# Another order of the same instructions: a product with a relu and a residual on one core

## The chip, the cores and the metric

The kernel runs on one core of one Trainium2 chip. The metric is the device time of one execution in microseconds; a kernel's time is the median of its runs. A core has five engines with queues of their own: TensorE (PE; PEld are its weight loads), VectorE (DVE), ScalarE (ACT), GpSimd (POOL), and SyncE (SP), which here only issues transfers. Each engine works through its queue in the order in which the program was written; between engines, semaphores hold an instruction until what it needs is there.

## What is computed

x has the shape (4, 1024, 512), W is (1536, 512), all in 32-bit floats. Cut to what matters:

```python
hidden = concatenate([cond, cond], axis=-1)          # (4, 512)
x_mean = mean(x, axis=1, keepdims=True)              # over 1024 rows
fused = concatenate([x, x_mean * ones_L, hidden[:, None, :] * ones_L], axis=-1)
out = x + relu(einsum('bld,do->blo', fused, W) + b)
```

So each of the four batch rows needs a product of its 1024 x 512 values with the first third of W, plus one bias vector per batch row: its mean times the second third of W, its condition times the last third, and b.

## The kernel before

**Tiles.** x is 32 tiles of 128 rows, eight per batch row. A tile needs 12 products: four slices of the inner dimension (j = 0 to 3), each with three products, because the 32-bit product is made of rounded parts: hi of x times hi of W, lo of x times hi of W, hi of x times lo of W (hi is the value cast to a rounded type, lo the difference that the cast left). Tiles are prepared in ten units: units 0 and 1 are one tile each, unit 2 has two tiles, all others four. Unit 4 holds tiles 8 to 11, unit 9 tiles 28 to 31.

**The order.** The program is a list of some 700 names, `ORDER` (lines 22 to 49), and each name is a task of one or a few instructions; line 437 goes through the list and issues them. Since each engine takes its instructions in that order, the list sets every queue. A letter behind @ picks the engine: d VectorE, a ScalarE, p GpSimd. The list was made by a search over orders with a plan of the times (a planner outside the kernel). The names:

- `X0.0`, `W0`, `C`, `B`, `M`, `V`, `Z4.0`: transfers into the chip, issued by SyncE one by one (line 145). X are tiles of x by rows, W0 and W1 the two halves of the first third of W, M and V the other thirds, C the condition, Z a unit of x laid out for VectorE's transposes.
- `T0.1`: a transpose, unit 0, slice 1. Units 0 to 3 are transposed by TensorE (line 244), the others by VectorE from Z (line 246).
- `h0.1`, `l0.1`: hi (line 252, ScalarE) and lo (line 258) of x. `wh1r`, `wl1r`: hi (lines 215 and 217) and lo (line 221) of W, slice 1, right half; without l or r, both halves.
- `p0.1.2`: tile 0, slice 1, product 2 of the three (line 348); `p9.2` stands for all three; `p31.1l` for the left half of tile 31.
- `K`, `b`, `r`, `F`: for tiles 0 to 17 the result is evicted from its bank of PSUM (K, ScalarE at line 415, VectorE at 423), the bias added (b, GpSimd), relu taken (r, ScalarE) and x added (F, GpSimd at line 431). For tiles 18 to 31 the bias is written into the bank first (P, ScalarE at lines 402 and 382) and F takes relu and adds x in one VectorE operation (lines 406 and 386). `S` stores a tile.
- `to`, `m`, `f`, `fa`, `vh`, `vl`, `pb`, `bc`, `g`, `d`, `as`: the bias of a batch row. `to` sums on GpSimd, `m` are four VectorE products with M, `f` ScalarE's copy after them, `pb` a product that sums over partitions, `bc` its copy.
- `fill`: products on zeros that keep TensorE busy before the first data.

**What holds what.** There are five banks for results: tile t uses bank t mod 5 (po_136 to po_140 in the lists below), so tile t + 5 can start only after the eviction of tile t. x's slots, lo buffers and parked results are reused in the same way. TensorE reads hi and lo of W from `w_hi` and `w_lo`, which are made at the start, from W0 (slices 0 and 1) and W1 (slices 2 and 3).

The loop that issues the tasks, and a cast and a difference of W:

```python
        @task(f"wh{j}{h}")
        def _(e, j=j, d=d):
            src, dst = xs[W_SLOT][:, j, d], w_hi[:, j, d]
            if e == "a":
                nc.scalar.activation(dst, src, AF.Copy)
            else:
                nc_of[e].tensor_copy(dst, src)
...
    for name in ORDER:
        if name == "fill":
            fill()
            continue
        name, _, engine = name.partition("@")
        tasks.pop(name)(engine)
```

Of the kernel before, what the change touches and what calls it, by code (L numbers as in the profile page):

```python
# [19 lines left out]


ORDER = """
relu X0.0 W0 X0.1 X0.2 W1 C B fill fill fill fill fill fill T0.0 T0.3 X1.0 T0.1 T0.2 X1.1 h0.0 V h0.1 l0.0@d
wh1r@d wh1l@a l0.1@d wh0l@a wl1r@p Z4.0 Z4.1 fill fill fill p0.1.0 wh0r@d h0.2 wl1l@d p0.1.1 h0.3 wl0l@p
wl0r@d p0.0.0 T1.0 l0.3@d T1.1 T1.3 T1.2 p0.0.1 p0.1.2 h1.0 T2.2 Z4.2 Z4.3 h1.2 T2.3 l1.0@d T2.0 h1.1 l1.2@d
p0.0.2 h2.3 p1.0.1 wh3@d p1.1.0 h1.3 T2.1 wh2@d h2.2 p1.1.2 wl3@p p1.0.2 wl2@d h2.0 Mb p1.0.0 p0.3.0 h2.1 Ma
p0.2.0 l0.2@d p1.2.0 l2.3@d p0.3.1 Z5.2 Z5.3 t3 p1.3.0 l1.1@d p1.2.2 l2.0@d p0.2.2 t2 p0.2.1 l2.1@d p1.3.2
l2.2@d p1.1.1 p0.3.2 t1 l1.3@d p1.2.1 t0 p2.3 T3.1 T3.0 h3.1 T3.3 ac0@p T3.2 h3.0 l3.1@d Z5.0 Z5.1 p2.1 K0@a
ac1@p h3.3 p3.0 g0.0 l3.3@d p1.3.1 p3.3 K1@a l3.0@d d0.0 Z6.2 Z6.3 p2.2 h3.2 p5.0 g0.1 l3.2@d g1.0 p3.1 d0.1
p6.1 T4.0 Z6.0 Z6.1 p6.3 d1.0 as0 T4.3 h4.0 p4.1 to0 T4.1 p3.2 g2.0 p2.0 K3@a m0.0 p5.2 h4.3 m0.1 p4.3 g1.1  # L30
T4.2 h4.1 p5.1 d1.1 K2@a p5.3 m0.2 Z7.0 Z7.1 h4.2 p6.0 l4.3@p m0.3 Z7.2 Z7.3 p7.3 l4.0@d f0 l4.1@p l4.2@d p6.2
g2.1 fa0 p4.2 d2.0 T5.1 vh0 p4.0 K5@a p8.2 vl0 h5.1 p7.1 T5.3 K6@a l5.1@p p8.1 T5.0 h5.3 p8.0 d2.1 K4@a pb0
T5.2 p10.0 h5.0 l5.3@p bc0@a p7.2 l5.0@d Z8.2 Z8.3 h5.2 p9.2 T6.1 as1 to1 X3.0 p11.1 b0@p Z8.0 Z8.1 m1.0 p8.3
T6.0 X5.1 b1@p p10.2 X2.1 K8@a m1.1 p9.3 h6.1 b3@p l5.2@d p11.2 r1 m1.2 p7.0 l6.1@p T6.2 p10.3 K7@a p13.2 h6.0
m1.3 b2@p p9.1 h6.2 T6.3 f1 p10.1 b5@p fa1 Z9.0 Z9.1 h6.3 p11.0 T7.1 vh1 p9.0 l6.3@p r5 p11.3 vl1 h7.1 p12.0
l6.0@d K9@a l7.1@p l6.2@d p12.2 K10@a r2 T7.3 p12.3 r0 pb1 T7.2 K11@a p13.0 F0 h7.3 p12.1 T7.0 bc1@a b4@p
p15.2 h7.2 K12@d p14.3 h7.0 T8.1 as2 p14.1 to2 F2 r3 p15.0 m2.0 r4 p16.3 m2.1 r12 b7@p S2 p13.3 X3.1 m2.2 S0
p17.1 l7.3@p m2.3 Z9.2 Z9.3 p14.2 l7.0@d f2 X5.0 p17.0 F4 l7.2@d g3.0 X2.0 p13.1 fa2 F1 p17.3 T8.0 vh2 p14.0
h8.1 vl2 F5 h8.0 p15.3 K13@d r7 p16.0 T8.3 l8.1@p S5 p16.1 X4.1 K14@d pb2 S1 d3.0 p16.2 T8.2 bc2@a p15.1 P18
l8.0@d F3 p17.2 g3.1 P19 p18.2 K17@d h8.3 d3.1 S3 p18.0 T9.1 X4.0 P22 p19.2 h8.2 l8.3@p T9.0 p19.0 r17 h9.1  # L40
p22.2 l8.2@d b10@p as3 p19.1 K15@d X6.1 T9.2 p22.0 P20 b6@p h9.0 p18.1 T9.3 h9.2 p18.3 K16@d p22.3 h9.3 F18
p19.3 P21 to3 b8@p m3.0 r10 S18 p22.1 P23 X6.0 m3.1 p20.2 r6 b11@p m3.2 p20.1 r15 r14 p23.3 m3.3 F6 p20.0 F22
f3 p21.3 l9.1@p fa3 p21.1 F19 vh3 F17 p23.1 vl3 p20.3 F7 p23.0 F20 pb3 p21.0 l9.3@p S7 bc3@a S19 p21.2 P27 S17
p23.2 F15 P25 S4 F21 r16 p27.2 F23 S21 P24 p27.1 S6 r13 l9.2@d p27.0 r8 l9.0@d P28 p27.3 F8 p25.0 F27 F16
p28.0 S8 P31r S15 P26 p25.2 X7.1 F10 p31.1r S22 p31.3r X7.0 p24.0 F12 p24.3 p25.3 b9@p S12 p31.0r p31.2r p24.2
F14 r9 p25.1 p24.1 F13 S14 p26.2 S10 F24 p26.3 F9 F25 P29 p26.0 F31r S25 P30 p29.2 S9 S31r p26.1 S27 p28.2 S20
F26 S23 p28.3 S26 P31l r11 p28.1 S24 F11 p29.1 F28 p29.3 S11 p30.0 S13 p30.3 S16 S28 p30.1 p30.2 p29.0 F30
p31.0l F29 p31.1l S30 p31.3l p31.2l S29 F31l S31l
""".split()


# [418 lines left out]
```

## Time and profile before

| | us |
|---|---|
| median of three runs | 104.49 |
| lowest and highest of them | 104.44, 106.45 |
| the profiled execution, its own time | 105.26 |
| its span, from the first to the last instruction | 103.5 |

The profile is of one execution, and its span leaves out what lies around the program. The granted clock of TensorE was 1.000 as a mean over the span. A group's row of the page names the line, the engine, the operation and what it writes and reads, then its count, busy time, mean length in ns, and the idle time ahead of it with what ended that. Busy shares are means over the whole span, and the start, the long middle and the end have different limits, so the windows and the timeline are needed too.

### The profile page before, as it was taken

Reading aid. Unit: us, or ns where it says so; the run is one execution under the profiler, and the core shown is the slowest. Engines: PE = TensorE matmul, PEld = TensorE weight load, DVE = VectorE, ACT = ScalarE, POOL = GpSimd, SP = SyncE. Lnnn points to the kernel's source line nnn. Section 1 sums busy time; section 2 is a strip of 40 time slices with the busy share of each in tenths; the row PEclk is TensorE's granted clock in tenths of the full one; section 3 lists DMA queues with packets and bytes.
Section 4 is the critical chain, followed back from the end, with each engine's and each line's share of the span. In section 5 each row is a group of like instructions: output and inputs, shape, how many; then the busy total and the mean of one; then the engine's idle time right before and its main releaser. Section 6 shows DMA issues by size and latency. Waiting matters only on the chain.

```text
span 103.5 us, 1434 instructions
## 1 busy us (share of the span) xinstructions
PE 97.6 (94%) x441; PEld 78.5 (76%) x441; DVE 73.1 (71%) x112; ACT 61.5 (59%) x153; POOL 71.6 (69%) x72
## 2 busy tenths in 40 slices
PE   6969989999999999999999999999999999999950
PEld 2538659888888888888888888888888888888850
DVE  1086992679999999999999999989948200622240
ACT  5156407969867956899937799887469302430000
POOL 4050507783797999997899999959997999705000
PEclk9999999999999999999999999999999999999999
DMA  1999999999999999999996999969209839999982
GB/s 51 285 332 407 411 234 209 215 326 201 210 216 209 203 208 199 197 155 244 244 180 146 344 234 393 402 219 344 101 17 371 328 108 278 331 403 405 401 331 77
DMA packets 22657, 26.31 MB, mean 254 GB/s; under 512 B 1269, under 2 KB 13817, under 8 KB 22650
## 3 DMA queue, kind: packets, MB, share of 16 engines
q1 hardware_dynamic: 22650, 26.23, 95.1%
q8 instruction: 3, 0.05, 0.2%
q14 instruction: 4, 0.03, 0.1%
HBM read 17.83 MB, written 8.39 MB: 253 GB/s over the span
## 4 chain that ended last, share of the span: by engine, by line
PE 83%; DVE 6%; DMA 5%; issue 2%; ACT 1%; SPq 0%; DVEq 0%
PE po L348 79%; DMA x<-in_L_cond_W_dram 5%; DVE lo L258 3%; DVE w_hi L217 2%; PE px L244 2%; ACT hi L252 1%; PE acc L326 1%; DVE cT L266 1%; PE po L244 0%; PE acc L244 0%; DVE x L386 0%; SPq L145 0%; DVE w_lo L221 0%; DVEq L258 0%
## 5 line engine op out<-in xcount | busy, mean ns | idle before, releaser
L348 PE MATMUL po<-w_hi,hi 128*128 128x512 f32 (+1 forms) x132 | 50.4, 385 | 0.9 <-ACT w_hi L215 0.7
L348 PE MATMUL po<-w_hi,lo 128*128 128x512 f32 (+1 forms) x132 | 50.8, 385 | 0.0
L348 PE MATMUL po<-w_lo,hi 128*128 128x512 f32 (+1 forms) x132 | 50.5, 385 | 0.1
L348 PEld LDWEIGHTS po<-w_hi,hi 128*128 128x128 f32 x132 | 24.8, 188 | 6.8 <-ACT w_hi L215 1.2
L348 PEld LDWEIGHTS po<-w_hi,lo 128*128 128x128 f32 x132 | 24.8, 188 | 5.0 <-DVE lo L258 0.3
L348 PEld LDWEIGHTS po<-w_lo,hi 128*128 128x128 f32 x132 | 24.7, 188 | 5.1 <-DVE w_lo L221 0.5
L431 POOL TENSOR_TENSOR x<-o,x 128x512 f32<-128x512 f32 x18 | 23.0, 1293 | 4.9 <-ACT o L427 4.9
L406 DVE SCALAR_TENSOR_TENSOR x<-po,x 128x512 f32<-128x512 f32 x13 | 8.8, 688 | 15.8 <-PE po L348 15.8
L258 POOL TENSOR_TENSOR lo<-xT,hi 128x512 fp32r<-128x512 f32 x12 | 15.5, 1298 | 0.9 <-ACT hi L252 0.9
L258 DVE TENSOR_TENSOR lo<-px,hi 128x512 fp32r<-128x512 f32 (+1 forms) x22 | 11.5, 537 | 6.5 <-ACT hi L252 6.5
L252 ACT ACTIVATE hi<-px 128x512 fp32r<-128x512 f32 (+1 forms) x22 | 10.4, 474 | 8.9 <-PE px L244 8.5
L419 POOL TENSOR_TENSOR o<-o,bias 128x512 f32<-128x512 f32 x12 | 15.3, 1295 | 0.0
L246 DVE STREAM_TRANSPOSE px<-z 128x512 f32<-128x512 f32 x12 | 13.0, 1098 | 0.7 <-DMA z<-in_x_dram 0.7
L427 ACT ACTIVATE o<-o 128x512 f32<-128x512 f32 x18 | 10.6, 620 | 4.3 <-POOL o L419 4.3
L246 DVE STREAM_TRANSPOSE xT<-z 128x512 f32<-128x512 f32 x12 | 12.9, 1086 | 0.1
L302 DVE SCALAR_TENSOR_TENSOR acc<-w_mean,tot,acc 128x512 f32<-128x512 f32 x16 | 11.8, 740 | 0.6 <-POOL tot L293 0.3
L402 ACT ACTIVATE po<-bias 128x512 f32<-128x512 f32 x13 | 7.6, 592 | 2.8 <-DVE x L406 2.2
L252 ACT ACTIVATE hi<-xT 128x512 fp32r<-128x512 f32 x12 | 7.5, 625 | 1.2 <-DVE xT L246 1.2
L415 ACT ACTIVATE o<-po 128x512 f32<-128x512 f32 x12 | 7.0, 589 | 1.9 <-PE po L348 1.8
L221 POOL TENSOR_TENSOR w_lo<-x,w_hi 128x256 fp32r<-128x256 f32 (+1 forms) x3 | 2.9, 968 | 7.0 <-DVE w_hi L217 7.0
L284 POOL TENSOR_TENSOR cond<-cond,term 128x512 f32<-128x512 f32 x4 | 5.2, 1297 | 2.8 <-ACT term L280 2.8
L280 ACT ACTIVATE term<-wc,cT 128x512 f32<-128x512 f32 x8 | 5.6, 719 | 0.1
(51 smaller groups left out, 71.9 us busy)
## 6 DMA issues: line engine op xcount, KB each, us to landing
out_dram<-x SPq DMA_DIRECT2D x31, 256.0 KB, 4.7
x<-in_x_dram SPq DMA_DIRECT2D x15, 512.0 KB, 6.9
z<-in_x_dram SPq DMA_DIRECT2D x24, 256.0 KB, 10.2
x<-in_L_cond_W_dram SPq DMA_DIRECT2D x2, 512.0 KB, 5.9
x<-in_L_cond_W_dram SPq DMA_DIRECT2D x1, 1024.0 KB, 10.3
w_mean<-in_L_cond_W_dram SPq DMA_DIRECT2D x2, 512.0 KB, 8.9
x<-in_x_dram SPq DMA_DIRECT2D x2, 256.0 KB, 4.1
out_dram<-x SPq DMA_DIRECT2D x2, 128.0 KB, 3.4
```

Source lines behind the costliest of these rows:

```text
L246: nc.vector.transpose(xT.rearrange("p (n t) -> p n t", t=Q), zs[z_of(u)][:, : n * NQ].rearrange("p n (a j) -> p n j a", j=J)[:, :, j])
L252: nc.scalar.activation(his[buf][:, col : col + m], xT, AF.Copy, accum_out=sums[:, r, j, s : s + 1])
L258: nc_of[e].tensor_tensor(los[buf][:, col : col + m], xT, his[buf][:, col : col + m].bitcast(F32), ALU.subtract)
L280: nc.scalar.activation(terms[k], wc[:, k], AF.Copy, scale=cT[:, k, r : r + 1])
L302: nc.vector.scalar_tensor_tensor(acc, w_mean[:, j, :], tot[:, r, j : j + 1], acc, ALU.mult, ALU.add)
L348: nc.tensor.matmul(v, lhsT=a[:, col : col + P], rhs=m, start=WAYS[t] != "I" and key not in done, stop=done.count(key) == 3 * J - 1, skip_g ...
L402: nc.scalar.activation(bank(t), biases[r], AF.Copy)
L406: nc.vector.scalar_tensor_tensor(x_tile(t), bank(t), 0.0, x_tile(t), ALU.max, ALU.add)
L415: nc.scalar.activation(o, bank(t), AF.Copy)
L419: nc_of[e].tensor_tensor(o, o, biases[r], ALU.add)
L427: nc.scalar.activation(o, o, AF.Relu)
L431: nc.gpsimd.tensor_tensor(x_tile(t), o, x_tile(t), ALU.add)
```

## The change

No task is added, taken away or altered. The list is another one: a new search was run whose plan keeps VectorE's casts and lo of W apart from GpSimd's operations, lets W land later, and keeps TensorE cold for longer. The first two rows of the list:

```diff
 ORDER = """
-relu X0.0 W0 X0.1 X0.2 W1 C B fill fill fill fill fill fill T0.0 T0.3 X1.0 T0.1 T0.2 X1.1 h0.0 V h0.1 l0.0@d
-wh1r@d wh1l@a l0.1@d wh0l@a wl1r@p Z4.0 Z4.1 fill fill fill p0.1.0 wh0r@d h0.2 wl1l@d p0.1.1 h0.3 wl0l@p
+relu X0.0 W0 X0.1 X0.2 C W1 X1.1 fill fill fill fill fill fill T0.2 T0.0 B T0.3 T0.1 X1.0 h0.0 V h0.1 l0.0@d
+wh1r@d wh1l@a l0.1@d h0.2 Z4.2 Z4.3 fill fill fill p0.1.0 wl1l@d h0.3 wh0r@d p0.1.1 wh0l@a T1.0 wl0l@d T1.1
...
 """.split()
```

Of engines, these tasks change: `wl1r`, `wl0l` and `wl3` go from GpSimd to VectorE, and `wh3` from VectorE to ScalarE. All else that changes is place in a queue.

**VectorE, the start.** x_63 is where W0 and W1 land; lo_89 and lo_90 are those of units 0 and 1, px_141 and px_142 their transposes. Before:

```order
L258 TENSOR_TENSOR lo_89<-px_141,hi_75 128x128
L217 CAST w_hi<-x_63 128x256
L258 TENSOR_TENSOR lo_89<-px_141,hi_75 128x128
L217 CAST w_hi<-x_63 128x256
L221 TENSOR_TENSOR w_lo<-x_63,w_hi 128x256 x2
L258 TENSOR_TENSOR lo_89<-px_141,hi_75 128x128
L258 TENSOR_TENSOR lo_90<-px_142,hi_76 128x128 x2
L217 CAST w_hi<-x_63 128x512 x2
L221 TENSOR_TENSOR w_lo<-x_63,w_hi 128x512
```

Now:

```order
L258 TENSOR_TENSOR lo_89<-px_141,hi_75 128x128
L217 CAST w_hi<-x_63 128x256
L258 TENSOR_TENSOR lo_89<-px_141,hi_75 128x128
L221 TENSOR_TENSOR w_lo<-x_63,w_hi 128x256
L217 CAST w_hi<-x_63 128x256
L221 TENSOR_TENSOR w_lo<-x_63,w_hi 128x256 x3
L258 TENSOR_TENSOR lo_90<-px_142,hi_76 128x128
L258 TENSOR_TENSOR lo_89<-px_141,hi_75 128x128
L266 STREAM_TRANSPOSE cT<-bias_118 32x64
L258 TENSOR_TENSOR lo_90<-px_142,hi_76 128x128
L217 CAST w_hi<-x_63 128x512
L221 TENSOR_TENSOR w_lo<-x_63,w_hi 128x512
```

All four pieces of lo from W0 are now VectorE's, and of the two 512-wide casts from W1 only one is left here.

**TensorE, the start.** po_136 and po_137 are the banks of tiles 0 and 1; the operations with term_123 are transposes, into px_142 those of unit 1 (T1), into acc and po_140 those of unit 2 (T2). Before:

```order
L348 MATMUL po_136<-w_hi,hi_75 128x512
L348 MATMUL po_136<-w_hi,lo_89 128x512
L348 MATMUL po_136<-w_hi,hi_75 128x512
L244 MATMUL px_142<-term_123,x_65 128x128 x4
L348 MATMUL po_136<-w_hi,lo_89 128x512
L348 MATMUL po_136<-w_lo,hi_75 128x512
L244 MATMUL acc<-term_123,x_65 128x128 x4
L244 MATMUL po_140<-term_123,x_65 128x128 x2
L348 MATMUL po_136<-w_lo,hi_75 128x512
```

Now:

```order
L348 MATMUL po_136<-w_hi,hi_75 128x512
L348 MATMUL po_136<-w_hi,lo_89 128x512
L244 MATMUL px_142<-term_123,x_65 128x128 x4
L348 MATMUL po_136<-w_hi,hi_75 128x512
L348 MATMUL po_136<-w_hi,lo_89 128x512
L244 MATMUL acc<-term_123,x_65 128x128 x4
L348 MATMUL po_137<-w_hi,hi_76 128x512
L244 MATMUL po_140<-term_123,x_65 128x128 x2
L348 MATMUL po_136<-w_lo,hi_75 128x512
L244 MATMUL po_140<-term_123,x_65 128x128 x2
```

T1 comes one product earlier, and T2 stands ahead of the first product with lo of W, where before one such product stood ahead of it; a product of tile 1 comes in between.

**VectorE at F18, the first of the one-step evictions.** xT and px are VectorE's transposes, o_107 and o_108 receive the evictions K16 and K17 (K16 the row of o_107), x_63 <- po_139 is F18. Before (K17 stands further ahead):

```order
L246 STREAM_TRANSPOSE px_142<-z_71 128x512
L246 STREAM_TRANSPOSE xT_121<-z_71 128x512
L423 TENSOR_TENSOR o_107<-po_137,bias_117 128x512
L406 SCALAR_TENSOR_TENSOR x_63<-po_139,x_63 128x512
L302 SCALAR_TENSOR_TENSOR acc<-w_mean,tot,acc 128x512 x4
```

Now:

```order
L246 STREAM_TRANSPOSE xT_121<-z_71 128x512
L246 STREAM_TRANSPOSE xT_120<-z_71 128x512
L406 SCALAR_TENSOR_TENSOR x_63<-po_139,x_63 128x512
L423 TENSOR_TENSOR o_108<-po_138,bias_117 128x512
L302 SCALAR_TENSOR_TENSOR acc<-w_mean,tot,acc 128x512
L423 TENSOR_TENSOR o_107<-po_137,bias_117 128x512
```

F18 now stands ahead of K17 and K16 instead of behind both. On TensorE the first product of tile 23, which uses F18's bank after P23 on ScalarE, moves from place 290 to place 253 among the products.

On SyncE, C goes ahead of W1. In the middle, the store S4 is followed by X2.1, X3.1, S5, X5.1, X6.0, S2, X7.0, S13 and X6.1; before, X2.1, X3.1, X5.1, X6.1 and X6.0 stood ahead of S4. The queue ends with S29, S26, S30, S28 and the two halves of tile 31's store (`S31r`, `S31l`); before, with S13, S16, S28, S30, S29 and `S31l`.

More of the change, by code (lines that the diff above doesn't have):

```diff
@@ L22 @@
 ORDER = """
-relu X0.0 W0 X0.1 X0.2 W1 C B fill fill fill fill fill fill T0.0 T0.3 X1.0 T0.1 T0.2 X1.1 h0.0 V h0.1 l0.0@d
-wh1r@d wh1l@a l0.1@d wh0l@a wl1r@p Z4.0 Z4.1 fill fill fill p0.1.0 wh0r@d h0.2 wl1l@d p0.1.1 h0.3 wl0l@p
-wl0r@d p0.0.0 T1.0 l0.3@d T1.1 T1.3 T1.2 p0.0.1 p0.1.2 h1.0 T2.2 Z4.2 Z4.3 h1.2 T2.3 l1.0@d T2.0 h1.1 l1.2@d
-p0.0.2 h2.3 p1.0.1 wh3@d p1.1.0 h1.3 T2.1 wh2@d h2.2 p1.1.2 wl3@p p1.0.2 wl2@d h2.0 Mb p1.0.0 p0.3.0 h2.1 Ma
-p0.2.0 l0.2@d p1.2.0 l2.3@d p0.3.1 Z5.2 Z5.3 t3 p1.3.0 l1.1@d p1.2.2 l2.0@d p0.2.2 t2 p0.2.1 l2.1@d p1.3.2
@@ L28 @@
[L28 to L47, printed above, removed]
@@ L48 @@
-p31.0l F29 p31.1l S30 p31.3l p31.2l S29 F31l S31l
+relu X0.0 W0 X0.1 X0.2 C W1 X1.1 fill fill fill fill fill fill T0.2 T0.0 B T0.3 T0.1 X1.0 h0.0 V h0.1 l0.0@d
+wh1r@d wh1l@a l0.1@d h0.2 Z4.2 Z4.3 fill fill fill p0.1.0 wl1l@d h0.3 wh0r@d p0.1.1 wh0l@a T1.0 wl0l@d T1.1
+wl1r@d T1.2 T1.3 p0.0.0 wl0r@d p0.0.1 Z4.0 Z4.1 h1.0 T2.3 h1.1 T2.2 p1.0.0 h1.2 l1.1@d T2.1 h2.3 l0.3@d p0.0.2
+t1 T2.0 wh3@a l1.0@d Ma p1.0.2 wh2@d p0.1.2 h1.3 p1.0.1 wl2@d h2.0 p1.1.1 p0.3.1 h2.2 p0.3.0 l0.2@d Mb p1.3.0
+t0 h2.1 t3 p0.2.2 l1.2@d Z5.0 Z5.1 p0.2.1 wl3@d p1.1.0 p1.2.2 p0.2.0 t2 l2.2@d p1.2.0 p1.1.2 l1.3@d p1.3.2
@@ new lines @@
+l2.3@d T3.0 l2.0@d p1.2.1 l2.1@d T3.3 p3.2 ac0@p T3.2 Z5.2 Z5.3 T3.1 h3.2 p2.3 ac1@p h3.1 p2.2 h3.3 l3.1@d
+p0.3.2 p2.1 h3.0 l3.2@d Z6.0 Z6.1 g0.0 p2.0 to0 l3.3@d l3.0@d p1.3.1 d0.0 p3.1 K2@a g0.1 p3.0 T4.3 K0@a Z6.2
+Z6.3 d0.1 p7.1 K1@a T4.0 p5.1 h4.3 p6.3 g1.0 T4.1 as0 p7.3 d1.0 h4.0 X3.0 m0.0 p3.3 h4.1 p5.0 m0.1 g2.0 p4.3
+m0.2 g1.1 d2.0 p6.1 T4.2 p4.2 l4.1@p m0.3 Z7.2 Z7.3 h4.2 p6.2 l4.0@d K3@a p4.1 X5.0 l4.3@p f0 l4.2@d p4.0 Z7.0
+Z7.1 fa0 p7.2 d1.1 T5.1 vh0 p5.2 K4@a vl0 p6.0 g2.1 T5.3 p5.3 X4.0 h5.1 p8.3 l5.1@p T5.2 K5@a p8.2 h5.3 T5.0
@@ new lines @@
+p9.0 h5.2 l5.3@p pb0 l5.2@d Z8.0 Z8.1 p9.2 bc0@a T6.1 d2.1 p7.0 as1 Z8.2 Z8.3 T6.3 p9.3 K6@a h5.0 p8.0 h6.3
+to1 p10.3 b1@p m1.0 K7@a p11.1 g3.0 T6.2 b5@p p10.0 h6.1 m1.1 p9.1 r1 l5.0@d h6.2 b7@p p8.1 m1.2 r5 p11.2 K8@a
+l6.2@d b0@p p11.3 m1.3 p11.0 T6.0 l6.3@p f1 p10.2 K11@a fa1 p12.0 Z9.0 Z9.1 r7 l6.1@p T7.3 h6.0 p10.1 p12.1
+l6.0@d d3.0 K10@a p12.3 T7.1 vh1 r0 p15.1 F5 vl1 K9@a p12.2 h7.3 T7.2 p14.2 F0 g3.1 T7.0 p15.3 h7.1 l7.3@p pb1
+S0 h7.2 p16.1 Z9.2 Z9.3 bc1@a l7.2@d p16.3 h7.0 K12@d p14.3 as2 to2 l7.0@d b2@p p14.1 m2.0 p15.2 m2.1 b3@p r2
@@ new lines @@
+p13.1 m2.2 p13.2 F2 r3 m2.3 p16.0 T8.0 f2 p14.0 F1 r12 fa2 p13.0 h8.0 T8.2 F3 p13.3 vh2 S1 p15.0 vl2 l7.1@p S3
+p17.2 K14@d h8.2 X4.1 p17.1 K13@d b4@p l8.2@d pb2 p17.0 T8.1 bc2@a p17.3 d3.1 P19 l8.0@d p16.2 P18 T8.3 r13
+b11@p p19.1 h8.1 p19.0 T9.2 h8.3 p18.3 r4 l8.3@p K15@d p18.1 as3 T9.0 P20 p18.0 l8.1@p T9.3 p18.2 h9.2 p20.0
+F4 r14 T9.1 p19.2 h9.0 F18 h9.3 p20.3 S4 K17@d h9.1 X2.1 p20.2 X3.1 P23 to3 p19.3 S5 b6@p m3.0 P22 X5.1 p23.2
+K16@d X6.0 p23.0 b10@p S2 m3.1 r16 p22.0 P21 m3.2 l9.1@p r15 p22.2 m3.3 r17 p21.1 f3 l9.3@p p22.3 fa3 X7.0
@@ new lines @@
+p23.3 F19 b8@p vh3 p22.1 r10 vl3 p23.1 r6 F13 F22 p21.2 pb3 F15 p20.1 S13 bc3@a X6.1 p21.3 P24 F20 F7 p21.0
+r11 F23 P27 p24.2 F21 r8 F6 S7 p27.0 P28 S19 p27.1 P25 b9@p S6 P26 p27.3 S21 X2.0 p25.1 F11 r9 S20 p25.0 p27.2
+F14 X7.1 p25.3 S18 F27 p25.2 F12 S14 l9.2@d P31r p24.3 l9.0@d F9 p24.1 F25 p31.0r P30 p31.1r F17 S9 p31.2r
+p31.3r S15 p30.0 S23 F8 p28.3 p24.0 F16 S8 p30.2 S12 F24 S25 p30.1 F31r F10 P29 S11 p30.3 S22 S17 p29.0 S16
+p26.3 S24 S27 p26.1 S10 p29.1 p29.2 p29.3 p26.0 F29 p26.2 S29 p28.0 F26 p28.1 F30 S26 P31l p28.2 S30 p31.3l
@@ L49 @@
+F28 p31.2l p31.1l p31.0l S28 S31r F31l S31l
 """.split()
```

## The prediction, made before the changed kernel was run

> **What bounds the kernel now.** I read the page first, then who waits on TensorE, then busy times by stretch, and last the timeline of the first 18 us.
>
> ```profile
> PE 97.6 (94%) x441; PEld 78.5 (76%) x441; DVE 73.1 (71%) x112; ACT 61.5 (59%) x153; POOL 71.6 (69%) x72
> PE 83%; DVE 6%; DMA 5%; issue 2%; ACT 1%; SPq 0%; DVEq 0%
> ```
>
> TensorE is the bound: 94% of the span, 83% of the chain that ended last. The waits on it, in total:
>
> ```profile
> PE acc L131 <- DVE one L123: 1.0, 1, 1.0
> PE po L348 <- ACT w_hi L215: 0.7, 1, 0.7
> PE px L244 <- DVE lo L258: 0.3, 1, 0.3
> PE po L348 <- DVE w_hi L217: 0.2, 1, 0.2
> ```
>
> All four lie before 16 us. The windows say the same (us of the stretch, then busy us and instructions of PE, PEld, DVE, ACT, POOL):
>
> ```profile
> 6.33:10.47 4.14, 3.93 (x22) 3.15 (x22) 3.32 (x9) 2.62 (x16) 1.50 (x3) 1.00 1.04 402
> 10.47:17.31 6.84, 6.46 (x35) 4.80 (x33) 5.29 (x14) 2.12 (x11) 2.40 (x2) 1.00 1.12 291
> 17.31:99.84 82.53, 82.52 (x377) 68.60 (x375) 62.82 (x84) 54.15 (x123) 66.34 (x61) 1.00 0.99 254
> 25.00:60.00 35.00, 35.00 (x156) 29.00 (x155) 34.59 (x45) 27.69 (x67) 31.18 (x29) 1.00 1.14 211
> ```
>
> From 17.31 to its end TensorE never stops, and VectorE is full from 25 to 60 us (34.59 of 35). From the chain of waits:
>
> ```profile
> 16.59 0.48 PE acc L244 x4
> 17.55 16.58 PE po L348 x73
> 99.86 0.42 DVE x L386
> ```
>
> A product takes 16.58 / 73 = 0.227 us, a transpose 0.48 / 4 = 0.12. Between the first product (6.33) and the 27th (17.31) stand 26 products and 28 transposes: 5.90 + 3.36 = 9.26 of 10.98 us. So 1.7 us are lost there, and that is all a better order can win; what lies ahead of 6.33 waits for W, whose transfers keep their places up to W0. After 99.84 come the last eviction, its store and the end.
>
> **The change, part by part.** (1) The casts and differences of W. VectorE and GpSimd in the timeline, and the three `w_lo` of VectorE (shortest, median, longest ns):
>
> ```profile
> 5.86 0.29 DVE L217 CAST w_hi<-x 128x256 fp32r<-128x256 f32 x1
> 6.24 1.47 POOL L221 TENSOR_TENSOR w_lo<-x,w_hi 128x256 fp32r<-128x256 f32 x2 [4.35 <-DVE w_hi L217]
> 6.27 0.85 DVE L217 CAST w_hi<-x 128x256 fp32r<-128x256 f32 x1
> 10.35 1.40 POOL L221 TENSOR_TENSOR w_lo<-x,w_hi 128x512 fp32r<-128x512 f32 x1 [2.64 <-DVE w_hi L217]
> 10.63 1.66 DVE L221 TENSOR_TENSOR w_lo<-x,w_hi 128x512 fp32r<-128x512 f32 x1
> L221 DVE TENSOR_TENSOR w_lo<-x,w_hi x3: 411/946/1664, 7.0 to 10.6; 128x256 fp32r<-128x256 f32 x2, 128x512 fp32r<-128x512 f32 x1
> ```
>
> The same cast takes 0.29 alone and 0.85 beside GpSimd; a 256-wide `w_lo` takes 0.41 at best. All three GpSimd pieces go to VectorE, and the cast wh3 to ScalarE. VectorE then pays two pieces of 0.41 and one of 512. No row shows that one alone: from below 0.66 (VectorE's 512-wide operations below), from above 2 x 0.41 = 0.82; I take 0.75, as it has the form of the 0.41. Free of GpSimd, VectorE saves 0.85 - 0.29, 0.95 - 0.41 and 1.66 - 0.75: 2.0 us, against 0.82 + 0.75 added and a 0.42 cast given away. It ends this stretch 0.8 us earlier; wh3 costs ScalarE about 0.6, between h2.3 and h1.3, where it sat idle.
>
> (2) TensorE's start, walked with these rows:
>
> ```profile
> 6.33 0.50 PE L348 MATMUL po<-w_hi,hi 128*128 128x512 f32 x1 [0.66 <-ACT w_hi L215]
> 6.67 0.40 PE L348 MATMUL po<-w_hi,lo 128*128 128x512 f32 x1
> 7.27 0.48 PE L348 MATMUL po<-w_hi,hi 128*128 128x512 f32 x1 [0.21 <-DVE w_hi L217]
> 7.59 0.63 PE L244 MATMUL px<-term,x 128*128 128x128 f32 x4
> 7.98 0.48 PE L348 MATMUL po<-w_hi,lo 128*128 128x512 f32 x1
> 8.29 0.40 PE L348 MATMUL po<-w_lo,hi 128*128 128x512 f32 x1
> 15.37 1.23 PE L244 MATMUL px<-term,x 128*128 128x128 f32 x8 [0.27 <-DVE lo L258]
> 17.31 0.48 PE L348 MATMUL po<-w_hi,hi 128*128 128x512 f32 x1
> ```
>
> They give the steps: product to transpose 0.32 (7.27 to 7.59), four transposes and on to a product 0.39, two 0.16, the first product after transposes 0.31, others 0.227. Two landings bind. Issues, and from their windows the time from issue to landing:
>
> ```profile
> 1.63 0.90 SPq L145 DMA_DIRECT2D x<-in_x_dram  x2
> 2.57 0.47 SPq L145 DMA_DIRECT2D x<-in_L_cond_W_dram  x1
> x<-in_x_dram SPq DMA_DIRECT2D x1, 512.0 KB, 6.2
> x<-in_L_cond_W_dram SPq DMA_DIRECT2D x1, 512.0 KB, 7.0
> ```
>
> X0.2 (the second of the pair, from 2.1) lands at 8.3, W1 at 9.6. C now goes ahead of W1: 4 KB and one issue of 0.4 us while the queue is full, so 0 to 0.4 on W1; I take 0.1.
> The new order: products at 6.33 and 6.67, T1 at 6.99, products at 7.38 and 7.69. T2.3 would come at 8.01, waits for X0.2 and comes at 8.36: 0.35 lost, new. Products at 8.75, 9.23, 9.71 and 10.02 with T2.1 and T2.0 between, then 13 in a row from 10.25 to 12.97, T3.0 at 13.29, a product at 13.68, T3.3 at 14.00, p3.2 from 14.39, T3.2 and T3.1 from 15.25, the 26th product at 16.25 and the 27th at 16.56. Against 17.31 that is 0.75 us. What must be ready is: wh3 at 9.7 + 0.6 = 10.3 for 10.70; wl2 at 9.7 + 0.42 + 0.75 = 10.9 for 11.39; wl3, after four short VectorE operations (1.1 us) and its 0.75, at 12.7 for 12.97. Should W1 land the full 0.4 later, these slip by 0.1 and the gain falls to 0.65.
>
> (3) What gives it back. VectorE's long run of work starts when the tile Z4 lands, and its transfers stand behind the same bytes as before:
>
> ```profile
> 21.78 1.10 DVE L246 STREAM_TRANSPOSE px<-z 128x512 f32<-128x512 f32 x1 [0.68 <-DMA z<-in_x_dram]
> 41.55 0.70 DVE L302 SCALAR_TENSOR_TENSOR acc<-w_mean,tot,acc 128x512 f32<-128x512 f32 x1
> 67.63 0.65 DVE L423 TENSOR_TENSOR o<-po,bias 128x512 f32<-128x512 f32 x1
> 68.20 0.68 DVE L406 SCALAR_TENSOR_TENSOR x<-po,x 128x512 f32<-128x512 f32 x1
> L402 ACT ACTIVATE po<-bias 128x512 f32<-128x512 f32 x13 | 7.6, 592 | 2.8 <-DVE x L406 2.2
> ```
>
> So VectorE keeps its clock while TensorE runs 0.75 ahead, and the order ties them closer in two places. First K10, which frees a bank for p15.1, only six products after tile 10's last: it stands on ScalarE behind f1, K11, r7 and h6.0, and f1 waits for m1.3. VectorE has one `lo` more ahead of m1.3 than before (42.25 + 0.6 = 42.85), and five ScalarE operations of 0.6 give 45.85. p15.1 is product 155: 17.31 + 128 x 0.227 = 46.37 before, 45.62 after the gain, so 0.2 goes back. Second F18, which frees a bank for P23 and so for p23.2. The order moves K17 and K16 behind it: 68.88 - 2 x 0.57 = 67.74, plus P23 at 0.59 is 68.33. p23.2 is product 253: 68.61 before, 67.86 after, so it waits and 0.28 of the gain is left (the first loss is inside this one). Elsewhere I found over 0.3 us to spare.
>
> (4) The end. The last store is `S31l`, 128 KB, in both orders, and its time to landing is
>
> ```profile
> out_dram<-x SPq DMA_DIRECT2D x1, 128.0 KB, 2.3
> ```
>
> S28 and S31r now come just ahead of it (384 KB) where two stores of 256 KB stood. I count 0, from -0.3 to +0.3.
>
> **Sum.** -0.75 + 0.2 + 0.27 + 0 = -0.28. The profiled execution took 105.26 (span 103.5 and 1.76 around it) and the median of the runs is 104.49, so 0.77 lower; -0.3 on it is 104.2, with a span of 103.2.
>
> **A page's rule.** The transposes at the start show the cold array, though the row of granted clock stands at full speed throughout:
>
> ```profile
> 0.97 2.74 PE L131 MATMUL acc<-warm 128*128 128x512 bf16 x6 [0.97 <-DVE one L123]
> 3.70 1.10 PE L244 MATMUL px<-term,x 128*128 128x128 f32 x4
> ```
>
> The six fills stand 0.42 apart ((2.74 - 0.63) / 5, the last alone 0.63), four transposes take 1.10 here and 0.63 at 7.59. My sum has the array warm by 6.33, as in this execution. If it stayed cold until X0.2 lands, four products at 0.42 for 0.227 and four transposes at twice 0.12 add 1.25; the new wait of 0.35 covers part, 0.9 stays. That is 105.1 (rival C). The Trainium skill ("TensorE: Matmul & The Clock Gate", "What's actually happening") says that about 3.4 us of activity switch the clock and that the window runs freely, so that one kernel warms up at another moment in each run. By that rule rival C would come now and then; here the array is warm 5 us after the first fill, and before would pay the same.
>
> **The rivals.** A: VectorE and GpSimd fall behind. to1 on GpSimd stands ahead of m1.0, behind l5.1 and l5.3 that wait for ScalarE's h5.1 and h5.3; by the rows I put it at 37.3 for a VectorE that gets there at 37.6. Whatever it is later goes whole into m1.3, F18 and p23.2, as VectorE has no idle time to absorb it. It decides from 0.6 us late: 0.3 of slack and 0.3 of gain. At 1.5 us late the end moves by 1.2 - 0.3 = +0.9: 105.4. For it speaks the full VectorE, against it that GpSimd is relieved of 2.9 us and has idle time ahead. B: nothing comes out. The start is better but another VectorE-paced bank takes the rest: 104.5. For it speaks the same row of 34.59. D: the gates at K10 and F18 don't hold, and all of 0.75 with a lighter end arrives: 103.5. For it speaks that both come out by under 0.5 us.
>
> **How the numbers follow.** The likeliest case has 0.5 (103.8 to 104.4 of its own), A 0.17, B 0.17, C 0.04, D 0.12. The range takes in A at 1.5 us and D with the end at its best: 103.3 to 105.4. 2% is 2.1 us, about what a measurement of this kernel can tell from no change. Faster by that needs more than the 1.7 us lost at the start: 0.02. Slower needs A at over 2.7 us: 0.07. Within: 0.91.
>
> **What would show it.** Right: no GpSimd `w_lo`, VectorE's casts near 0.29 and 0.42, the 27th product near 16.6, a new wait of TensorE for X0.2 near 8, small waits at p15.1 and p23.2. Wrong: `w_lo` on VectorE still near 0.9, the 27th product past 17, or waits of TensorE for a `po` eviction that add up to over 0.7 us.

## The result, and the profile after

| | before | after |
|---|---|---|
| median of the runs on one chip, us | 105.03 (104.44 to 106.45, 6 runs) | 108.52 (107.16 to 111.94, 6 runs) |
| the profiled execution, us | 105.26, span 103.5 | 111.94, span 110.2 |

After takes 1.0305 of before (95% interval 1.0234 to 1.0375): slower, by some 3.2 us, where 104.2 was forecast. Ratios leave out the executions that took over 1.5% more than the fastest of the same kernel, so 1.0305 is not the quotient of the two medians, and among the profiled executions those of after, of before again, of both runs with Z7 and Z8 first and of the second run of after's start are such long ones. The profiled execution of after is 3.4 us longer than its median, so its waits are probably larger than in the others; a second profile, on another chip, comes with the experiments.

The page of after: busy times, the row of granted clock in 40 slices, and the shares of the chain that ended last.

```profile
PE 99.8 (91%) x441; PEld 79.5 (72%) x441; DVE 72.2 (65%) x114; ACT 62.5 (57%) x154; POOL 68.8 (62%) x69
...
PEclk9999999999999999999679999999999999999995
...
PE 48%; DMA 27%; POOL 5%; SPq 5%; issue 4%; DVE 4%; ACT 3%; DVEq 0%; POOLq 0%
```

TensorE's share of the chain fell from 83 to 48%, and DMA's rose from 5 to 27%: something waits for transfers. TensorE was also granted less than its full clock in two slices in the middle. The longest waits of TensorE in after, in total:

```profile
PE acc L326 <- DVE v_acc L322: 2.1, 1, 2.1
PE po L348 <- ACT o L415: 1.4, 2, 0.9
PE px L244 <- DMA x<-in_x_dram: 1.0, 1, 1.0
```

The first row is new and large: `pb1`, the product that sums over partitions for the bias of the second batch row, waits for VectorE's `vl1`. The windows of after, the first three from the first product to the 27th and on to the end, then the stretch in which VectorE had been full, then the one with the low clock:

```profile
6.18:10.47 4.29, 3.17 (x16) 2.29 (x17) 2.55 (x10) 2.26 (x13) 0.00 (x0) 1.00 1.02 396
10.47:17.28 6.81, 6.81 (x40) 6.01 (x39) 4.57 (x14) 2.54 (x12) 0.61 (x1) 1.00 1.11 316
17.28:105.70 88.42, 85.00 (x375) 69.34 (x373) 63.39 (x84) 55.17 (x125) 66.88 (x61) 0.98 0.96 231
25.00:60.00 35.00, 31.58 (x130) 24.88 (x129) 29.92 (x39) 25.25 (x59) 26.71 (x25) 0.95 1.18 192
53.20:56.60 3.40, 3.29 (x8) 2.61 (x9) 3.37 (x6) 2.35 (x8) 0.37 (x2) 0.50 1.21 210
```

From the 27th product on, 82.53 us became 88.42: TensorE stood still for 3.42 of it and its busy time on the same products was 2.48 longer. The 3.42 are the 2.06 of `pb1` and two evictions on ScalarE, 0.44 for K6 near 39 us and 0.92 for K10, for which p15.1 waits:

```profile
48.15 0.50 PE L348 MATMUL po<-w_hi,hi 128*128 128x512 f32 x1 [0.92 <-ACT o L415]
```

VectorE, busy 34.59 of 35 us before, was busy 29.92. The chain of after names what it waited for:

```profile
36.70 13.04 DMA z<-in_x_dram
...
49.86 1.10 DVE xT L246
50.96 0.57 DVE lo L258
...
52.58 0.69 DVE v_acc L322
...
53.31 0.79 PE acc L326
54.11 10.79 PE po L348 x42
```

A load of 256 KB (Z7.1, the last of unit 7) took 13.04 us from issue to landing. T7.3 on VectorE waits for it and starts at 49.86; `l6.0` and T7.1 follow, and `vl1` behind them ends at 53.27. SyncE's issues in that stretch, first before, then after:

```profile
25.72 10.67 SPq L145 DMA_DIRECT2D z<-in_x_dram  x8
36.43 1.14 SPq L145 DMA_DIRECT2D x<-in_x_dram  x1
37.61 1.85 SPq L145 DMA_DIRECT2D z<-in_x_dram  x2
```

```profile
30.11 1.77 SPq L145 DMA_DIRECT2D x<-in_x_dram  x1
32.00 2.12 SPq L145 DMA_DIRECT2D z<-in_x_dram  x2
34.22 1.70 SPq L145 DMA_DIRECT2D x<-in_x_dram  x1
35.97 2.91 SPq L145 DMA_DIRECT2D z<-in_x_dram  x2
38.97 1.89 SPq L145 DMA_DIRECT2D x<-in_x_dram  x1
```

Before, all of Z7 and half of Z8 go out before the first of these x loads. After, X3.0 stands ahead of Z7, X5.0 in the middle of it, and X4.0 between Z7 and Z8. Each is 512 KB, and the residual that it brings isn't needed until its tile is finished. They are in a queue that is full (DMA share over 1), and Z7's last piece landed at 49.73 us in place of 40.59.

Counting the products (line 348, without `pb`) in each trace gives the table below; the tiles named are those of after's order. In it, *again* is the same kernel in a second profile; the last two columns are experiments told below.

| start of product, us | before | after | after, again | Z7, Z8 first, again | and stores by readiness |
|---|---|---|---|---|---|
| 27 | 17.31 | 17.28 | 16.33 | 16.32 | 16.42 |
| 155 (in p15.1) | 46.66 | 48.49 | 45.59 | 45.58 | 45.68 |
| 180 | 52.55 | 58.38 | 51.49 | 51.47 | 51.58 |
| 253 (just behind p23.2) | 69.33 | 75.16 | 69.24 | 68.26 | 68.37 |
| 396, the last | 99.55 | 105.42 | 99.48 | 98.47 | 98.64 |
| from 27 to 396 | 82.24 | 88.14 | 83.15 | 82.15 | 82.22 |
| issue of the last store | 100.31 | 106.85 | 101.07 | 100.65 | 99.41 |
| end of the span | 103.5 | 110.2 | 104.4 | 104.5 | 102.2 |
| this execution, us | 105.26 | 111.94 | 106.16 | 106.29 | 103.96 |

Counted in this way, the first product of tile 23 moves from place 259 to place 250; with the `pb` ahead of it these are 262 and 253, so the 290 given above for before is too high.

The 5.9 us that the first profile of after loses between product 27 and the last lie in two stretches: 1.9 up to product 155, where the two evictions are waited for, and 4.0 from there to product 180, where `pb1` waits. After again loses nothing up to product 180 and 0.98 from there to 253.

### The profile page after: what moved, and what is told of

Same layout as the page of the kernel before. It is cut to its first block, busy times and chain, and to the rows that moved or that the text cites. A ratio compares the mean times of both kernels' runs of the same rounds, so it can differ in the third digit from the quotient of the medians.

```text
span 110.2 us, 1432 instructions
## 1 busy us (share of the span) xinstructions
PE 99.8 (91%) x441; PEld 79.5 (72%) x441; DVE 72.2 (65%) x114; ACT 62.5 (57%) x154; POOL 68.8 (62%) x69
## 4 chain that ended last, share of the span: by engine, by line
PE 48%; DMA 27%; POOL 5%; SPq 5%; issue 4%; DVE 4%; ACT 3%; DVEq 0%; POOLq 0%
PE po L348 46%; DMA z<-in_x_dram 21%; DMA x<-in_x_dram 6%; SPq L145 5%; POOL lo L258 4%; DVE xT L246 2%; ACT hi L252 2%; POOL cond L284 2%; PE acc L326 1%; ACT term L280 1%; DVE v_acc L322 1%; DVE lo L258 1%; ACT acc L297 0%; DVE x L386 0%; DVEq L246 0%
## 5 line engine op out<-in xcount | busy, mean ns | idle before, releaser
L348 PE MATMUL po<-w_hi,hi 128*128 128x512 f32 (+1 forms) x132 | 51.6, 393 | 1.8 <-ACT o L415 1.4
L348 PEld LDWEIGHTS po<-w_hi,hi 128*128 128x128 f32 x132 | 25.3, 192 | 8.3 <-ACT o L415 2.4
L274 POOL TENSOR_TENSOR wc<-x 128x512 f32<-128x512 f32 x2 | 2.5, 1296 | 14.8 <-DMA x<-in_L_cond_W_dram 14.8
L402 ACT ACTIVATE po<-bias 128x512 f32<-128x512 f32 x13 | 7.4, 590 | 5.3 <-DVE x L406 5.2
L284 POOL TENSOR_TENSOR cond<-b_sb,term 128x512 f32<-128x512 f32 x4 | 5.2, 1297 | 2.9 <-ACT term L280 2.9
L382 ACT ACTIVATE po<-bias 128x256 f32<-128x256 f32 x2 | 0.8, 390 | 8.8 <-DVE x L406 8.8
```

What stands on the lines that cost most here:

```text
L284: nc.gpsimd.tensor_tensor(conds[r % 2], conds[r % 2] if k else b_sb, terms[k], ALU.add)
L348: nc.tensor.matmul(v, lhsT=a[:, col : col + P], rhs=m, start=WAYS[t] != "I" and key not in done, stop=done.count(key) == 3 * J - 1, skip_g ...
L402: nc.scalar.activation(bank(t), biases[r], AF.Copy)
```

## The experiments

Ratios are to the kernel before, timed on the same chip in the same rounds, with their 95% interval. The experiments ran on three chips; the unchanged kernel took 104.7 to 104.8 on each.

| kernel | chip | median, us | ratio |
|---|---|---|---|
| after, again | A | 106.4 | 1.0129 (1.0073 to 1.0186) |
| after, Z7 and Z8 first | A | 105.56 | 1.0056 (1.0018 to 1.0095) |
| before, X3.0 and X5.1 early | A | 106.1 | 1.0119 (1.0069 to 1.0170) |
| before, four engine letters | A | 104.0 | 0.9951 (0.9913 to 0.9988) |
| before, again | B | 104.82 | 1.0012 (0.9978 to 1.0046) |
| after, Z7 and Z8 first, again | B | 105.16 | 1.0019 (0.9988 to 1.0049) |
| after, besides stores by readiness | B | 104.34 | 0.9946 (0.9920 to 0.9972) |
| start of after, rest of before | B | 104.27 | 0.9920 (0.9880 to 0.9961) |
| the same, again | C | 103.92 | 0.9899 (0.9860 to 0.9937) |
| the same, W1 ahead of C | C | 104.66 | 0.9941 (0.9900 to 0.9983) |
| after, X4.0 earlier | C | 109.06 (108.07 to 111.54) | 109.06 / 104.68 = 1.042, no interval |
| besides, vl1 ahead | C | 108.03 | 1.0292 (1.0234 to 1.0351) |

**After, again.** No edit.

> The changed kernel as it is, for a second profile. Theory Q (SyncE's queue: the loads of X3, X5 and X4 now stand ahead of or between the four loads of Z7 and those of Z8, Z7 lands some 6 us later than before, the transpose T7.3 on VectorE waits for it, the addition vl1 stands behind T7.3, and TensorE's first output product waits for vl1): about 108, with a wait of 1.5 to 3 us of VectorE's transposes for z near 47 to 50 us and a wait of 1 to 2 us of TensorE's product-sum for v_acc near 53 us. Theory S (the loss comes of the start and of the engines that were exchanged): about 108 too, but with the wait spread over the stretch up to 45 us.

It took 106.4, not 108. The loads came faster in this execution, and neither theory's wait is there in full. VectorE in this execution, around Z7's landing:

```profile
42.80 0.67 DVE L314 TENSOR_TENSOR acc<-acc,fold 64x512 f32<-64x512 f32 x1
44.29 1.13 DVE L246 STREAM_TRANSPOSE xT<-z 128x512 f32<-128x512 f32 x1 [0.82 <-DMA z<-in_x_dram]
45.34 0.64 DVE L258 TENSOR_TENSOR lo<-px,hi 128x512 fp32r<-128x512 f32 x1
45.91 1.10 DVE L246 STREAM_TRANSPOSE xT<-z 128x512 f32<-128x512 f32 x1
47.04 0.69 DVE L322 TENSOR_TENSOR v_acc<-acc,v_acc 64x512 fp32r<-64x512 f32 x1
```

T7.3 starts at 44.29 and `vl1` ends 3.44 later, as in the first profile (49.86 and 53.27: 3.41). It ends at 47.73, and `pb1` starts at 48.09 without a wait: Z7 landed just soon enough. But the 0.82 us that VectorE lost are not forgotten. The second sum's `vl2` comes late, so that the product behind `pb2` starts 0.36 later than in the runs without this wait, and p20.0 loses 0.4 to P20 on ScalarE, which follows VectorE's K15. The gain of the start, 0.98 us at product 27, is 0.09 at product 253. Then the last store is issued 1.59 us behind the start of the last product, where before it was 0.76. Neither theory had foreseen that.

**Z7 and Z8 first.** SyncE's queue alone:

```diff
 Z6.2 Z6.3
-X3.0
 Z7.2 Z7.3
-X5.0
 Z7.0 Z7.1
-X4.0
 Z8.0 Z8.1 Z8.2 Z8.3
+X3.0 X5.0 X4.0
 Z9.0 Z9.1
```

> The changed kernel with the loads of X3.0, X5.0 and X4.0 moved in SyncE's queue to right behind the last load of Z8; the order of every other engine is that of the changed kernel. Theory Q: 104.0 to 105.0, with no wait of TensorE for v_acc and none over 1 us of VectorE for z beyond 45 us. Theory S: 107.5 to 108.5, since nothing of the start nor of the engines' letters is touched.

> The same kernel as in the run with Z7 and Z8 first, for a comparison on one chip with the run with the stores by readiness, and for a second profile. Theory Q: 104.8 to 105.6, no wait of TensorE behind the 28th product, and the last store issued 0.7 to 1.0 us behind its tile.

The median fell from 1.0129 to 1.0056 of before on one chip (the intervals just overlap) and was 1.0019 on the next. Q expected 104.0 to 105.0 of the first run: 105.56 is above that, S's 107.5 further off. The trace is plainer than the time. In the second profile, the window from the 27th product to the end has TensorE busy throughout:

```profile
16.32:98.75 82.43, 82.43 (x375) 68.46 (x373) 63.26 (x84) 54.90 (x125) 66.37 (x61) 1.00 0.94 245
```

Three loads moved on SyncE, and the whole loss of the middle is gone: 82.43 us against 82.53 in the kernel before. The run with the stores sorted, which has the same three loads moved, shows the same in an execution of 103.96 us (82.22 from product 27 to 396). What is left stands at the end: the last store goes out 1.44 us behind its tile in the second profile, where Q had said 0.7 to 1.0; it was 0.90 in the first, and 0.85 in after again.

**Two x loads early, in the kernel before.** The converse:

```diff
 Z6.0 Z6.1
+X3.0
 Z7.0 Z7.1
+X5.1
 Z7.2 Z7.3 Z8.2 Z8.3
-X3.0
 Z8.0 Z8.1
-X5.1
 X2.1
```

> The kernel before with only two loads moved in SyncE's queue: X3.0 ahead of the loads of Z7, and X5.1 between them, as the changed kernel has it. Theory Q: 106.5 to 108.5, with the wait for v_acc. Theory S: 104.5 to 105.3, as before.

1.0119, 106.1: a little under Q's range and well over S's. Nothing else was touched, so these two places alone cost as much as the whole change does on this chip. That the two are equal is chance, since the change also wins 1.0 at the start and loses 0.8 at the end. Its waits on TensorE have the row that before doesn't:

```profile
PE acc L326 <- DVE v_acc L322: 0.4, 1, 0.4
```

By the starts of the products, 0.2 us go at `pb1` and 0.64 at `pb2`, of 1.3 that are lost from product 27 to the last.

**The four letters alone, in the kernel before.** `wl1r`, `wl0l`, `wl3` to VectorE, `wh3` to ScalarE:

```diff
-wl1r@p wl0l@p wl3@p wh3@d
+wl1r@d wl0l@d wl3@d wh3@a
```

> The kernel before with only four operations given to other engines: the three subtractions wl1r, wl0l and wl3 from GpSimd to VectorE, the cast wh3 from VectorE to ScalarE; no row of the order is moved. My first step (VectorE's casts and subtractions get shorter when GpSimd leaves them alone, and the 27th product comes up to 0.75 us earlier): 104.0 to 104.8. Theory S: 105.5 or more, if the letters themselves cost. Theory Q says nothing of it: 104.2 to 105.2.

0.9951, at the lower bound of what was expected; the 27th product came at 16.59 us, 0.72 ahead of before. VectorE's pieces of W in this kernel:

```profile
L221 DVE TENSOR_TENSOR w_lo<-x,w_hi 128x256 fp32r<-128x256 f32 x4 | 1.5, 418 | 0.0
L221 DVE TENSOR_TENSOR w_lo<-x,w_hi 128x512 fp32r<-128x512 f32 x2 | 1.3, 688 | 0.2 <-ACT w_hi L215 0.2
L217 DVE CAST w_hi<-x 128x256 fp32r<-128x256 f32 x2 | 0.6, 290 | 0.2 <-DMA x<-in_L_cond_W_dram 0.2
```

The cast takes 0.29 where it took 0.85 beside GpSimd, and the 512-wide difference 0.69 for 1.66. The Trainium skill ("SBUF — State Buffer", "Who interferes with whom") says that VectorE and GpSimd share one pair of ports as an exclusive lock, which a cast in a two-port mode takes, and that an operation with two inputs in SBUF contends with GpSimd's reads; 0.29 against 0.85 and 0.69 against 1.66 agree. The theory that the letters themselves cost falls.

**Stores by readiness.** The end of SyncE's queue, on top of Z7 and Z8 first:

```diff
-S2 X7.0 S13 X6.1 S7 S19 S6 S21 X2.0 S20 X7.1 S18 S14 S9 S15 S23 S8 S12 S25 S11 S22 S17 S16
-S24 S27 S10 S29 S26 S30 S28 S31r S31l
+S2 S18 X7.0 S13 X6.1 S22 S20 S15 S7 S19 S6 X2.0 S21 S23 X7.1 S27 S11 S14 S12 S25 S9 S24 S17
+S31r S8 S16 S10 S29 S26 S30 S28 S31l
```

> The changed kernel with X3.0, X5.0 and X4.0 behind Z8, as in the run with Z7 and Z8 first, and besides with the stores from S18 on (and X7.1, X2.0) put in SyncE's queue in the order in which the profile of the changed kernel showed their tiles ready; the order of all other engines is that of the changed kernel. Theory Q, widened (the stores stand in an order in which those not yet ready hold up those long ready, so nine of them go out back to back at the end, 0.69 us each, and the last leaves 0.85 us late): 103.9 to 104.7, some 0.8 us less than with Z7 and Z8 first alone, the last store issued within 0.1 us of its tile. Theory R (the end is long since VectorE's or GpSimd's last operations come later): no gain on the run with Z7 and Z8 first, 105.0 to 105.7.

0.9946 against 1.0019 on the same chip: 0.76 us, as expected, and R falls. The last eviction and the last store, first with Z7 and Z8 first, then with the stores sorted too:

```profile
98.58 2.66 SPq L145 DMA_DIRECT2D out_dram<-x  x4
...
98.79 0.42 DVE L386 SCALAR_TENSOR_TENSOR x<-po,x 128x256 f32<-128x256 f32 x1 [0.74 <-PE po L348]
```

```profile
98.95 0.42 DVE L386 SCALAR_TENSOR_TENSOR x<-po,x 128x256 f32<-128x256 f32 x1 [0.74 <-PE po L348]
...
99.41 0.33 SPq L145 DMA_DIRECT2D out_dram<-x  x1
```

Four stores leave in one run of 2.66 us, some 0.69 apart, and the last of them, ready at 99.21, goes out last, at 100.65. With the stores sorted it follows its tile at once (99.37 to 99.41). Where the backlog comes from shows in after itself: S4 waits for its tile, and SyncE issues nothing from 63.81 to 72.77 us. The window 68 to 72 of before, then of after (the last two numbers are DMA share and GB/s):

```profile
68.00:72.00 4.00, 4.00 (x19) 3.34 (x18) 3.62 (x6) 3.66 (x8) 3.31 (x5) 1.00 0.77 250
```

```profile
68.00:72.00 4.00, 4.00 (x20) 3.30 (x19) 4.00 (x6) 3.74 (x10) 3.09 (x3) 1.00 0.00 0
```

X2.1, X3.1 and X5.1 wait for no store and could have gone in that time, and all that was held up meets the stores of the last tiles.

**The kernel before, again.**

> The kernel before as it is, for a second profile on the chip of these runs: 104.4 to 105.2, no wait of TensorE behind the 28th product, the 27th product between 16.5 and 17.4 us, and the span's end 3.3 to 4.0 us behind the start of the last product.

1.0012, the same kernel. Its profile missed what was expected of it: the 27th product came at 17.72, and TensorE waits 0.33 us for an eviction and 1.5 us near 73 us for a bias (ScalarE, L402), of which no other profile has more than 0.14. Its last store is issued 3.5 us later than in the first profile of before. So the first profile stays the one that after is compared with.

**The start of after before the rest of before.** The 27 products and all that stands around them are from after's list, the rest is in before's order.

> The start of the changed kernel, up to its 27th product, with its engines, in front of the rest of the kernel before in that one's order (Z4, Z5 in the order of before too). My second step (the whole start is worth 0.75 us): 103.6 to 104.2, the 27th product some 0.7 to 1.0 us ahead of before's. If the start of the changed kernel is worth no more than the exchanged engines alone: 104.0, as that run. If C ahead of W1 or the later T2 cost more than they bring: 104.3 or more.

> The kernel with the start of the changed one before the rest of the kernel before, again, for a comparison on one chip with W1 ahead of C and for a second profile: 0.988 to 0.996 of before, the 27th product at 16.3 to 16.9 us depending on when X0.1 lands.

0.9920 and 0.9899: both ahead of before with their whole intervals, by less than 1.5%, and the best here. The first run's 104.27 lies just outside the 103.6 to 104.2 of the second step and just below the 104.3 of the last theory; the ratio of the second run was expected. The start is worth 0.8 to 1.1 us, of which the letters alone gave 0.5 on another chip. The 27th product came at 16.87 and 17.12 in the two profiled executions, both later than expected and than the 16.33 of after again, in the main because in both TensorE waited for X0.1 (0.31 and 0.63 us), which the new order asks for one product earlier; the first product was also slower in both (0.57 and 0.54 us to the second, for 0.33).

**W1 ahead of C.** In that kernel:

```diff
-C W1
+W1 C
```

> The run with the start of the changed kernel before the rest of the kernel before, with C again behind W1 on SyncE. My second step had C ahead of W1 cost 0 to 0.4 us, taken at 0.1: 0 to 0.4 us less than the run with the start of the changed kernel on the same chip. If W1 isn't what ends the start's waits: the same within 0.1.

0.9941 against 0.9899: no gain where 0 to 0.4 us was expected, and the intervals overlap. That C ahead of W1 costs anything isn't shown.

**X4.0 earlier, in after.**

```diff
 X5.0
+X4.0
 Z7.0 Z7.1
-X4.0
 Z8.0
```

> The changed kernel with one load more ahead of Z7's last two: X4.0 from behind Z7.1 to behind X5.0. Theory Q (the landing of Z7.1 sets vl1 some 3.5 us later, and vl1 sets TensorE's first product of the sum): Z7.1 lands 2 us later than in the changed kernel, TensorE waits 1.5 to 2.5 us for v_acc at that product, and the whole takes 1.5 to 4 us more than the changed kernel on the same chip (106.4 in the run again), the upper part if the clock falls to half after the wait. Theory S (loads in the middle are covered): no more than 0.3 us more.

109.06 against 104.68 of before on its chip. Its two shorter runs took 108.07 and 108.33, some 2.0 us more than the three shorter runs of after again; by the medians it is 2.7. Both are within Q's 1.5 to 4, but the two kernels were timed on different chips. The chain of this kernel:

```profile
33.73 12.90 DMA z<-in_x_dram
...
46.75 1.11 DVE xT L246
...
49.47 0.70 DVE v_acc L322
...
50.21 0.55 PE acc L326
```

One more load ahead, Z7.1 lands 2.46 us later than in after again (46.63 for 44.17), `vl1` ends 3.41 behind T7.3's start once more, and `pb1` waits 2.00 us.

**vl1 ahead, on top of that.** Of VectorE's order:

```diff
+vl1
 T7.3 l6.0@d T7.1
-vl1
```

> As the run with X4.0 earlier, with vl1 on VectorE moved ahead of T7.3, l6.0 and T7.1, so that it no longer stands behind the transposes that wait for Z7. Theory Q with the queue as its cause (what costs is only that vl1 stands behind T7.3): no wait at the first product of the sum, 105.5 to 106.8. Theory V (VectorE has no time to spare from 44 to 70 us, so what it loses to a transpose's wait comes out at its next result that TensorE needs): the wait moves to the second product of the sum near 57 to 60 us or to a result bank, and the time stays within 1 us of the run with X4.0 earlier.

108.03: Q's range ended at 106.8. V had the wait at the second sum right; the time is 1.03 below the other median, where V gave 1 us, and within 0.3 of that kernel's two shorter runs. VectorE and TensorE's second sum in this kernel, from the timeline:

```profile
45.64 0.68 DVE L322 TENSOR_TENSOR v_acc<-acc,v_acc 64x512 fp32r<-64x512 f32 x1 [1.75 <-ACT v_acc L318]
47.38 1.09 DVE L246 STREAM_TRANSPOSE xT<-z 128x512 f32<-128x512 f32 x1 [1.06 <-POOL x L431]
...
59.45 0.69 DVE L322 TENSOR_TENSOR v_acc<-acc,v_acc 64x512 fp32r<-64x512 f32 x1
```

```profile
60.19 0.77 PE L326 MATMUL acc<-v_acc,ones 128*128 128x512 f32 x1 [2.01 <-DVE v_acc L322]
60.76 0.63 PE L348 MATMUL po<-w_hi,hi 128*128 128x512 f32 x1
61.19 0.63 PE L348 MATMUL po<-w_hi,lo 128*128 128x512 f32 x1
```

The first sum no longer waits, the second waits 2.01 us. By this run the queue decides only where the loss comes out. VectorE stood idle for 1.75 and 1.06 us and then has work without a pause until `vl2`, so what it lost comes out there. The second of these the profile puts down to GpSimd, but it ends 0.12 after the landing of Z7.1 (47.26), as T7.3's wait does in after again (44.17 and 44.29). The test isn't a clean one, since `vl1` now waits for ScalarE; but the time that VectorE lost is about the same in both kernels (2.8 and 3.3 us), and so is the wait of TensorE.

## Why the prediction was wrong

- **What bounds the kernel** was right, and so was the warning in it: VectorE has 34.59 of 35 us full. The runs say it again: most of what VectorE lost came out as a wait of TensorE.
- **(1), the pieces of W**: right. 0.29 for the cast, 0.69 for the 512-wide difference (0.75 was taken), 0.42 for the others; the letters alone brought the 27th product 0.72 ahead, of which 0.12 is an earlier first product.
- **(2), the start**: right in kind, with the new wait for X0.2 (0.18 us in after again, 0.35 expected), and somewhat larger in size: the 27th product at 16.33 and 16.42 us (16.56 expected) when X0.1 lands in time. In the first profile of after X0.1 landed at 7.86 us for 6.94, T1 waited 1.0 us for it, and the gain was 0.03. The walk had X0.2 and W1 as the two landings that bind; X0.1 is a third.
- **(3), what gives it back**: here the prediction failed, in the sentence that VectorE keeps its clock since "its transfers stand behind the same bytes as before". That holds for Z4, from whose landing it was concluded, and not for Z7, which stands behind up to 1 MB more. I counted VectorE's instructions and the two banks, K10 and F18. The loads that were moved, X3.0 and X5.0 ahead of Z7's last piece and X4.0 behind it, I named neither ahead of the prediction, where only the loads around S4 stand, nor in it, so their places in SyncE's queue were put at nothing. With Z7 and Z8 first neither bank makes TensorE wait: K10 ended at 44.79 us (45.85 was worked out) and P23 at 67.39 (68.33), so the terms of 0.2 and 0.27 were 0. The term that was left out is 0.9 us in after again (0.98 gained at product 27, 0.07 left at the last product). In the first profile it is at most the 4.0 of product 155 to 180. The 1.9 ahead of them follow on loads that were late before any moved one (VectorE waited 1.64, 1.18 and 0.33 us for Z4, Z5 and Z6), and there the bank of K10 did bind, by the path of the prediction (m1.3, f1, K11, r7, h6.0, K10), with 0.92 for 0.2. The two evictions add up to 1.36, over the 0.7 that was named as a sign of being wrong.
- **(4), the end**: counted at 0, within 0.3; it costs 0.8 us. I compared the last three stores and not the queue ahead of them.
- **The sum**: -1.0 at the start, +0.9 in the middle and +0.8 at the end make +0.7 for after again against the profiled execution of before; its time is 0.9 more. On the first chip the profiled execution of after lost 5.9 in the middle; how the 3.2 us of the medians divide there no profile shows.
- **Rival A** had the right engine and in the main the wrong cause: VectorE fell behind for the landing of Z7. GpSimd's `to1` did make m1.0 wait in after again:

```profile
36.95 0.76 DVE L302 SCALAR_TENSOR_TENSOR acc<-w_mean,tot,acc 128x512 f32<-128x512 f32 x1 [0.43 <-POOL tot L293]
```

With Z7 and Z8 first that wait was 0.29 and TensorE lost nothing by it, so `to1` alone does not explain the 0.9; how much of it the wait of 0.43 added no run separates.
- **Rival C** did come, in one execution. The products of the first profile with Z7 and Z8 first:

```profile
6.71 0.80 PE L348 MATMUL po<-w_hi,hi 128*128 128x512 f32 x1 [0.86 <-ACT w_hi L215]
7.30 0.63 PE L348 MATMUL po<-w_hi,lo 128*128 128x512 f32 x1
7.73 1.05 PE L244 MATMUL px<-term,x 128*128 128x128 f32 x4
...
9.43 0.91 PE L244 MATMUL acc<-term,x 128*128 128x128 f32 x4
10.10 0.48 PE L348 MATMUL po<-w_hi,hi 128*128 128x512 f32 x1
```

From the first to the fifth product it takes 3.39 us, against 2.46 in after again: 0.93, where 0.9 was worked out. In both profiles of after the array was warm by the first product, so nothing shows that this has a part in the result.

**What stays open.** Why the transfers were slower in the first profile than in the second. Of the 4.0 us there from product 155 to 180, 2.06 are the wait of `pb1` and the rest comes with the halved clock behind it (last section), which a landing only 2.46 us later than in after again was enough to cause with X4.0 earlier. But Z7.1 landed 5.56 us later than in after again, and Z5.3 and Z6.2, ahead of any of the moved loads, were late too (32.28 and 36.87 us, 28.70 and 32.78 in after again). Whether that is the chip or the execution no run here tells, and the runs with loads moved were not made on the first chip; the order explains why late transfers hit this kernel, not why they were late.

## What to carry to other kernels

When an order changes, walk the DMA queue like any engine: for every load that a busy engine waits for, add up the bytes that now stand ahead of it, and move what is needed late (a residual) behind what is needed soon. On an engine without idle time a wait doesn't vanish in a later gap: here it reached the bound engine at the next result that this one needs, and moving that result ahead moved the wait to the next. Let stores stand in the order in which their tiles become ready, since here one that waited left the transfers idle and made a backlog for the end.
